# A macaron block in fp32: measures of later tiles, output-weight sums, token sums, one closing step and the last tile are each put elsewhere

## The chip, the cores and the metric

The kernel runs on one core of a Trainium2 chip. The metric is the device time of one execution in microseconds (us). Before the change three runs took 773.85, 774.33 and 774.45 us, median 774.33. The profile is one further execution of the same kernel.

Engines are named as in the profile: PE is the matrix engine TensorE (PEld its weight loads), DVE is VectorE, ACT is ScalarE, POOL is GpSimd, SP issues the DMAs. Each works through its own queue in order; they wait for one another through semaphores.

## The reference

`x` is 4 sequences of 256 tokens with 512 features, 1024 tokens in all. The block adds half a feed-forward, attention, and half a feed-forward again, each behind its own layer norm; both feed-forwards have the same weights.

```python
def _L0_attn_ref(x, wq, wk, wv, wo):       # 32 query heads, 8 key/value heads of 128
    q = (x @ wq).reshape(B, S, N_Q_HEADS, HEAD_DIM)
    k = (x @ wk).reshape(B, S, N_KV_HEADS, HEAD_DIM)
    v = (x @ wv).reshape(B, S, N_KV_HEADS, HEAD_DIM)
    q = _rope(q, pos); k = _rope(k, pos)
    scores = jnp.einsum('bqhgd,bshd->bhgqs', qg, k) * sm_scale
    allowed = (j <= i) & (j > i - SLIDING_WINDOW)          # window of 128
    attn = jax.nn.softmax(jnp.where(allowed, scores, neg), axis=-1)
    out = jnp.einsum('bhgqs,bshd->bqhgd', attn, v)
    return out.reshape(B, S, -1) @ wo

def _L0_ffn_ref(x, W_base, b_base, W_router, lora_A, lora_B):   # 8 experts of rank 16, top 2
    probs = softmax(xf @ W_router.T)
    w = one_hot(top 2) * (their probs, normed to a sum of 1)
    lora_out = jnp.einsum('ter,eor,te->to', h, lora_B, w) * SCALING   # h = xf by lora_A
    return x @ W_base.T + b_base + lora_out

x = x + 0.5 * ffn(layernorm(x))
x = x + attn(layernorm(x))
x = x + 0.5 * ffn(layernorm(x))
```

## The kernel before, in words

The 1024 tokens are 8 tiles of 128 rows. Tiles 0 to 3 (two sequences) are half 0 and tiles 4 to 7 half 1. All arithmetic is fp32. The rows `xt[t]` stay in SBUF from the first load to the last store.

*The first feed-forward* (`ffn`, called for both halves as `halves[0]` and `halves[1]`) is written as steps named by a letter and a tile of the half: M measures the mean and variance of a tile (`measure`: a statistics and an aggregate operation on DVE, a square root on ACT), X scales the rows with them (`scale`: on ACT in this feed-forward, on DVE in the others), T transposes them (`norm`: four transposes on PE, one copy on ACT), N does X and T, A multiplies by the adapters and the router, R computes the experts' shares, B is the base matmul of a tile into a PSUM bank (`base`, four matmuls of 512 columns), G gates the adapters, L leaves: the last matmul, by the adapters' second half, and an update of the tile on DVE (`leave`, L355 and L356). H and K are B's first and second two matmuls. A leave calls `then(t)`: in the first feed-forward `norm_later`, which measures the tile anew for the attention's norm and notes half 1's tiles in `behind`; in the second feed-forward `store`, which sends the tile out by a DMA on SP (L751).

*The projections* for q, k, v and the output use a scheme of seven products in place of eight (Strassen's, in Winograd's form). Each operand is cut in four quarters, sums of the quarters are made ahead, and products go into shared PSUM banks with additions on DVE between them. Sums of weights are made on POOL, four operations for each weight: `sum_weights` for q, k and v (L121) and `sum_o_weights` for the output (L126). Sums of tokens, `sum_tokens`, are four operations (L400), for half 0 on DVE and for half 1 by POOL and DVE in turn. Weight tiles and their sums (`wq`, `wqs`, `wos` and so on) have one buffer each, or two for `wo`, so new sums overwrite old ones.

`queries` gives the seven products of q as steps "1" to "7". A finished quarter goes through `rope`: one operation on DVE with the cosine (L380, tile `ra`), two with the sine (L382, tile `rb`), and a closing addition on POOL (L388). `ra` and `rb` have two buffers. With a list as `later`, the closing addition isn't issued but put on that list. Product 3's is always put on the list `ends` and issued by the caller later; product 5's was issued at once. `keys` and `project_values` do the same for k and v, in four parts called first, both, second and others.

*The attention* runs over 16 groups (half, key/value head), each with two units (one for each sequence of the half), 32 units in all. A unit u transposes its probabilities (L640), computes the scores of the unit after it (`scores`, L587 and L601), multiplies by v (`values`, L662), and starts the exponentials of the unit after (`exponentials`, L616 to L623). The four output products of a unit (`outputs`, L688, added on DVE at L698 and L705) are put on the queue `late` and worked off within the next unit. `normalize` (a reciprocal at L629 on DVE, two multiplications at L632 on POOL) closes a softmax. In units with b = 0 a string gives the order in which the seven products of the next group's q ("1" to "7") alternate with other steps ("n" normalize, "y" one of `late`, "t" transposes, "w" the output-weight sums, "v" and "k" early work of the first unit). Units with b = 1 do the k or v products for a following group, and the left-over work of half 1's norm: in every second such unit `scale` and `norm_attn` for the next two tiles of `behind`. Value units, those whose b = 1 part finishes v, are the ones with even n (n is the group's index plus 1).

*The second feed-forward* of half 0 runs in pieces inside the last units of half 1 (`fill`, `loose`); that of tiles 4 to 7 ends the program. The last line of orders reads:

```python
        (1, "N1 A0 A1 R"), (0, "G L0 L1"), (1, "B0 G H1 L0 K1 L1"),
```

Here number 1 is the pair of tiles 6 and 7, so the last tile's base matmul is cut in two, tile 6's leave stands between, and tile 7's leave, its update and its DMA are the program's end.

*What sets the order.* ACT and POOL run in the order in which the code is written, all through. So do PE and DVE until three units are left; the rest of theirs is ordered by a scheduler. So moving a call moves its instructions in the queue of every engine that it uses, and a wait of the first in a queue holds the rest. PSUM has four banks for matmuls (`mm_bank`) and four for scores and transposes (`score_bank`). Ahead of the first tile PE runs idle transposes of an identity (L166) until there is work.

The lines around the first feed-forward's end, which the change reorders:

```python
    tokens = sum_tokens(0, *(nc.vector,) * 4)
    for step in (1, 2, 3, 4):
        tokens[step]()
    sum_weights("k", *groups[0])
    sum_weights("q", *groups[0])
    for step in "L0 L1 B3".split():
        halves[1](step)
    first, both, second, others = keys(*groups[0])
```

Of the kernel before, what the change touches and what calls it, by code (L numbers as in the profile page):

```python
# [13 lines left out]
AF = mybir.ActivationFunctionType  # L14
ALU = mybir.AluOpType
# [23 lines left out]
def macaron_kernel(  # L39
# [122 lines left out]
    make_identity(nc, ident)  # L162

    idle = ps.tile([P, KC, P], F32, tag="s", bufs=4, name="idle")
    for n in range(21):
        nc.tensor.transpose(idle[:, n % KC, :], ident, ident)  # L166


# [68 lines left out]
    def scale(t, tag):  # L237
        if (tag, t) not in moments:
            measure(t, tag)
        mv, std = moments[tag, t]  # L240
        rstd = sb.tile([P, 1], F32, tag="rstd", bufs=4, name=f"rs_{tag}_{t}")
        nc.vector.reciprocal(rstd, std)
        xc = sb.tile([P, D], F32, tag="xc", bufs=3, name=f"xc_{tag}_{t}")
        if tag == "f1":
            shift = sb.tile([P, 1], F32, tag="shift", bufs=4, name=f"sh_{tag}_{t}")
            nc.vector.scalar_tensor_tensor(shift, mv[:, 0:1], -1.0, rstd, ALU.mult, ALU.mult)
            nc.scalar.activation(xc, xt[t], AF.Identity, bias=shift, scale=rstd)
        else:
            nc.vector.tensor_scalar(xc, xt[t], mv[:, 0:1], rstd, ALU.subtract, ALU.mult)
        moments[tag, t] = xc  # L250
# [49 lines left out]
    def ffn(tiles, tag, then):  # L300
        n, t0 = len(tiles), tiles[0]
        xf, po, state = {}, {}, {}

        def x_of(i, c):
            return xf[i // 2][:, c, ts(i % 2, P)]

        def enter(i, scaled=False):
            if i % 2 == 0:
                xf[i // 2] = sb.tile(
                    [P, KC, 2 * P], F32, tag="oT", bufs=4, name=f"xn_{tag}_{tiles[i]}"  # L310
                )
            norm(tiles[i], xf[i // 2], i % 2, tag, scaled)

        def look(i):
            measure(tiles[i], tag)

        def shape(i):
            scale(tiles[i], tag)

        def turn(i):  # L320
            enter(i, scaled=True)

        def narrow(i):
            t = tiles[i]
            if i == 0:
                state["hl"] = sb.tile([P, TPH, E * R + E], F32, tag="hl", name=f"hl_{tag}_{t0}")[:, :n, :]
            pa = score_bank(f"pa_{tag}_{t}")
            for c in range(KC):
                nc.tensor.matmul(  # L329
                    pa[:, : E * R + E], x_of(i, c), ar_sb[:, c, :],  # L330
                    start=(c == 0), stop=(c == KC - 1),
                )
            nc.scalar.copy(state["hl"][:, i, :], pa[:, : E * R + E])
            nc.gpsimd.tensor_tensor(xt[t], xt[t], half_bias, ALU.add)

        def shares():
            route(t0, n, state["hl"], tag)

        def base(i, chunks=range(KC)):
            if chunks[0] == 0:  # L340
                po[i] = mm_bank(f"po_{tag}_{tiles[i]}")
            for c in chunks:
                nc.tensor.matmul(po[i], x_of(i, c), wb_sb[:, c, :], start=(c == 0), stop=False)  # L343

        def gated():
            hl = state["hl"]
            pt = ps.tile([P, n, P], F32, tag="s", bufs=4, name=f"ph_{tag}_{t0}")
            for i in range(n):
                nc.tensor.transpose(pt[:, i, :], hl[:, i, : E * R], ident)
            state["ht"] = sb.tile([P, TPH, P], F32, tag="ht", bufs=1, name=f"ht_{tag}_{t0}")  # L350
            nc.scalar.copy(state["ht"][:, :n, :], pt)

        def leave(i):
            out, t = po.pop(i), tiles[i]
            nc.tensor.matmul(out, state["ht"][:, i, :], lb_sb, start=False, stop=True)  # L355
            nc.vector.scalar_tensor_tensor(xt[t], out, 0.5, xt[t], ALU.mult, ALU.add)  # L356
            then(t)

        steps = {
            "M": look, "X": shape, "T": turn, "N": enter, "A": narrow, "R": shares, "G": gated,  # L360
            "B": base, "H": lambda i: base(i, range(KC // 2)), "K": lambda i: base(i, range(KC // 2, KC)),
            "L": leave,
        }
        return lambda s: steps[s[0]](*(int(i) for i in s[1:]))

# [44 lines left out]
    def temp(name, at):  # L410
        return sb.tile([HD, TH], F32, tag=name, bufs=1, name=f"{name}_{at}")

    def queries(h, g, copy, later=None):

        state = {}

        qT[h, g] = sb.tile([HD, BPH, S // BLK, G, BLK], F32, tag="qT", name=f"qT_{h}_{g}")  # L420

        def product(n, bank=None):
            w, x = weights["qs", h, g][n - 1], xs[h][n - 1]
            new = bank is None
            if new:
                bank = mm_bank(f"q{n}_{h}_{g}")
            for j in range(2):
                for c in range(2):
                    nc.tensor.matmul(  # L429
                        bank[:, ts(j, S)], w[:, c, ts(j, HD)], x[:, c, :],  # L430
                        start=(new and j == 0 and c == 0), stop=(c == 1), skip_group_check=True,
                    )
            return bank

        def turn(b, j, src, later=None):
            rope(
                qT[h, g][:, b, :, j : j + 2, :], src, f"q_{h}_{g}_{b}_{j}",
                lambda t: t.rearrange("p (j e q) -> p e j q", j=2, q=BLK), later,
            )

        def first():
            state["p1"] = product(1)
            state["p1c"] = temp("p1c", f"q_{h}_{g}")
            copy(state["p1c"], state["p1"])

        def sixth():
            state["p6"], state["u2"] = product(6), temp("u2", f"q_{h}_{g}")
            add(state["u2"], state["p6"], state["p1c"])

        def seventh():  # L450
            state["p7"], state["v1"] = product(7), temp("v1", f"q_{h}_{g}")
            add(state["v1"], state["p7"], state["u2"])

        def fifth():
            state["p5"] = product(5)
            add(state["p6"], state["p5"], state["v1"])
            turn(1, 2, state["p6"])

        def second():
            turn(0, 0, product(2, state["p1"]))

        def fourth():
            bank = product(4, state["p7"])
            add(bank, bank, state["u2"])
            turn(0, 2, bank)

        def third():
            product(3, state["p5"])  # L470
            add(state["p5"], state["p5"], state["u2"])
            turn(1, 0, state["p5"], later)

        return {"1": first, "2": second, "3": third, "4": fourth, "5": fifth, "6": sixth, "7": seventh}
# [284 lines left out]
    def norm_later(t):  # L759
        if t >= TPH:  # L760
            behind.append(t)
        measure(t, "a")

# [16 lines left out]
    for h, order in (  # L782
        (0, "M0 M1 X0 X1 T0 T1 M2 A0 X2 M3 A1 T2 X3 B0 T3 A2 A3"), (1, "M0 M1 X0 X1"), (0, "B1"),
        (1, "T0 T1 M2 M3 X2"), (0, "R B2"), (1, "X3 T2"), (0, "B3"), (1, "T3"), (0, "G"),
        (1, "A0 A1 A2 A3"), (0, "L0 L1"), (1, "R"), (0, "L2 L3"), (None, "X0 X1 X2"), (1, "B0 B1 B2"),
        (None, "T0 T1 X3"), (1, "G"), (None, "T2 T3"),
    ):
        for step in order.split():
            (attn if h is None else halves[h])(step)
    tokens = sum_tokens(0, *(nc.vector,) * 4)  # L790
    for step in (1, 2, 3, 4):
        tokens[step]()
    sum_weights("k", *groups[0])
    sum_weights("q", *groups[0])
    for step in "L0 L1 B3".split():
        halves[1](step)
    first, both, second, others = keys(*groups[0])
    ends = []
    steps = queries(*groups[0], nc.scalar.copy, ends)
    first()  # L800
    both()
    for step in "L2 L3".split():
# [7 lines left out]
        if step == "4":  # L810
            load_q(*groups[1])
    sum_weights("q", *groups[1])
    ends.pop()()
    load_o(*groups[1])


# [24 lines left out]
    for u, (h, g, b) in enumerate(units):  # L841
# [12 lines left out]
        if b == 0 and n < len(groups):  # L854

            order = {0: "1n6kv2754t3w", 4: "1yn6a27cy5d4yte3yw"}[len(late)]
            steps = queries(*groups[n], nc.vector.tensor_copy, ends)
            steps |= {  # L860
                "y": lambda: run(late, 1), "n": lambda: normalize(ahead[0], ahead[2]),
# [12 lines left out]
        elif b == 1 and n + 1 < len(groups):  # L874
# [4 lines left out]
                more_tokens[4]()  # L879
            second()  # L880
            normalize(ahead[0], ahead[2])
            if n % 2 == 1 and (h, g) != groups[NKV]:
                sum_weights("v", *groups[n + 1])
            others()
            fill(left, 4)
            turned = [behind.popleft() for _ in range(2 if behind and n % 2 == 0 else 0)]
            for t in turned:
                scale(t, "a")
            if n % 2 == 0 and n + 2 < len(groups):
# [58 lines left out]
    f2 = [ffn(tiles(last[0], b, 1), "f2", store) for b in range(BPH)]  # L948
    for n, order in (
        (0, "N0 N1"), (None, 0), (None, 1), (0, "A0 A1 R B0"), (1, "N0"), (0, "B1"),  # L950
        (1, "N1 A0 A1 R"), (0, "G L0 L1"), (1, "B0 G H1 L0 K1 L1"),
    ):
        if n is None:
            out_project(*last, order, oT)
# [49 lines left out]
```

## Time and profile before

| | |
|---|---|
| median of three runs | 774.33 us |
| profiled execution | 773.88 us |
| its span, first to last instruction | 772.2 us |
| granted TensorE clock | 1.00 all through |
| idle transposes of PE at the start | to about 6.3 us |
| first base matmul (L343) | 10.89 us |
| first product of q (L429) | 58.56 us |
| first output product (L688) | 105.27 us |
| end of the last update on DVE | 769.18 us |
| last DMA: issue, first packet, landing | 769.21, 770.03, 771.21 us |

Times are read from the start of the span. An engine's row in the timeline gives the start, the duration, the engine and the line of the code, the operation with its tiles (out<-in), and in brackets how long the engine had been idle and what released it. A count behind an x means that so many instructions are drawn together. Part 6 of the page gives, for the DMAs, the time from issue to landing: 7.6 us for the base weights of 1024 KB, 5.5 for each q weight of 1024 KB, 2.0 for each output tile of 256 KB.

### The profile page before, as it was taken

Reading aid. Unit: us, or ns where it says so; the run is one execution under the profiler, and the core shown is the slowest. Engines: PE = TensorE matmul, PEld = TensorE weight load, DVE = VectorE, ACT = ScalarE, POOL = GpSimd, SP = SyncE. Lnnn points to the kernel's source line nnn. Section 1 sums busy time; section 2 is a strip of 40 time slices with the busy share of each in tenths; the row PEclk is TensorE's granted clock in tenths of the full one; section 3 lists DMA queues with packets and bytes.
Section 4 is the critical chain, followed back from the end, with each engine's and each line's share of the span. In section 5 each row is a group of like instructions: output and inputs, shape, how many; then the busy total and the mean of one; then the engine's idle time right before and its main releaser. Section 6 shows DMA issues by size and latency. Waiting matters only on the chain.

```text
span 772.2 us, 10908 instructions
## 1 busy us (share of the span) xinstructions
PE 764.5 (99%) x3809; PEld 617.4 (80%) x3809; DVE 538.7 (70%) x1307; ACT 213.9 (28%) x746; POOL 502.6 (65%) x540
## 2 busy tenths in 40 slices
PE   8999999999999999999999999999999999999998
PEld 6658888888888888888888888888888888877654
DVE  4487785857785877668677858586867768485673
ACT  5530232322223031322222232222141212223442
POOL 5452786866867595859585789669575957475411
PEclk9999999999999999999999999999999999999999
DMA  9301130303030302212030403030302011010001
GB/s 303 134 1 54 36 102 1 136 2 109 28 110 28 107 30 63 75 55 82 20 118 1 135 2 110 28 110 28 110 28 85 25 56 55 1 55 28 1 28 54
DMA packets 29335, 48.95 MB, mean 63 GB/s; under 512 B 1120, under 2 KB 10080, under 8 KB 29280
## 3 DMA queue, kind: packets, MB, share of 16 engines
q1 hardware_dynamic: 29280, 48.26, 18.5%
q8 instruction: 30, 0.49, 0.3%
q14 instruction: 25, 0.20, 0.1%
HBM read 46.15 MB, written 2.10 MB: 62 GB/s over the span
## 4 chain that ended last, share of the span: by engine, by line
PE 92%; DVE 4%; POOL 1%; issue 1%; ACT 0%; DMA 0%; DVEq 0%; POOLq 0%
PE y L688 24%; PE q L429 24%; PE ob L662 7%; PE k L486 6%; PE v L536 6%; PE po_f L343 5%; PE sb L601 4%; PE t L640 4%; PE sa L587 3%; PE oa L662 3%; PE pa_f L329 2%; PE po_f L355 1%; PE pt_f L258 1%; PE y L730 1%; DVE x L356 1%
## 5 line engine op out<-in xcount | busy, mean ns | idle before, releaser
L388 POOL TENSOR_TENSOR qT<-ra_q,rb_q 128x512 f32<-128x512 f32 x64 | 81.3, 1271 | 117.2 <-DVE rb_q L382 117.2
L382 DVE TENSOR_TENSOR rb_q<-q,sin_sb 64x512 f32<-64x512 f32 x128 | 88.1, 688 | 1.7
L644 ACT COPY p<-t 128x512 f32<-128x512 f32 x32 | 18.8, 586 | 212.9 <-PE t L640 212.9
L632 POOL TENSOR_TENSOR probs<-probs,sm 128x512 f32<-128x512 f32 x64 | 65.2, 1039 | 11.2 <-DVE sm L629 10.6
L688 PE MATMUL y<-wos,oT 128*128 128x256 f32 x248 | 63.9, 380 | 0.3 <-POOL wos L126 0.3
L688 PE MATMUL y<-wo,oT 128*128 128x256 f32 x248 | 63.7, 379 | 0.0
L688 PE MATMUL y<-wo,oTs 128*128 128x256 f32 x244 | 62.6, 379 | 0.0
L429 PE MATMUL q<-xs,wqs 128*128 128x256 f32 x256 | 60.6, 379 | 0.4 <-POOL wqs L121 0.4
L429 PE MATMUL q<-xs,wq 128*128 128x256 f32 x256 | 60.6, 379 | 0.2 <-DVE rb_k L382 0.2
L429 PE MATMUL q<-xa,wq 128*128 128x256 f32 x256 | 60.6, 379 | 0.0
L662 PE MATMUL ob<-p,v 128*128 128x512 f32 x128 | 60.2, 592 | 0.0
L380 DVE TENSOR_TENSOR ra_q<-q,cos_sb 128x512 f32<-128x512 f32 x64 | 44.3, 692 | 21.7 <-PE q L429 15.7
L429 PEld LDWEIGHTS q<-xa,wq 128*128 128x128 f32 x256 | 48.4, 190 | 12.8 <-issue 6.2
L343 PE MATMUL po_f<-wb_sb,xn_f 128*128 128x512 f32 x128 | 57.5, 593 | 0.0
L665 ACT COPY oT<-oa 128x512 f32<-128x512 f32 x32 | 18.7, 585 | 135.5 <-PE oa L662 135.5
L429 PEld LDWEIGHTS q<-xs,wqs 128*128 128x128 f32 x256 | 48.6, 190 | 7.4 <-POOL wqs L121 0.8
L429 PEld LDWEIGHTS q<-xs,wq 128*128 128x128 f32 x256 | 48.6, 190 | 7.1 <-issue 0.5
L688 PEld LDWEIGHTS y<-wo,oT 128*128 128x128 f32 x248 | 46.6, 190 | 6.0
L688 PEld LDWEIGHTS y<-wo,oTs 128*128 128x128 f32 x244 | 46.4, 190 | 6.3
L688 PEld LDWEIGHTS y<-wos,oT 128*128 128x128 f32 x248 | 45.6, 190 | 6.9 <-issue 1.0
L121 POOL TENSOR_TENSOR oTs<-oT 128x256 f32<-128x256 f32 x31 | 22.6, 731 | 40.6 <-ACT oT L665 40.5
L662 PEld LDWEIGHTS ob<-p,v 128*128 128x128 f32 x128 | 24.3, 190 | 30.6 <-issue 23.0
(182 smaller groups left out, 1711.5 us busy)
## 6 DMA issues: line engine op xcount, KB each, us to landing
wq<-in_wq_dram SPq DMA_DIRECT2D x16, 1024.0 KB, 5.5
wo<-in_wo_dram SPq DMA_DIRECT2D x16, 1024.0 KB, 5.0
wk<-in_wk_dram SPq DMA_DIRECT2D x8, 512.0 KB, 3.5
wv<-in_wv_dram SPq DMA_DIRECT2D x8, 512.0 KB, 3.5
x<-in_x_dram SPq DMA_DIRECT2D x8, 256.0 KB, 6.9
out_dram<-x SPq DMA_DIRECT2D x8, 256.0 KB, 2.0
wb_sb<-in_w_base_dram SPq DMA_DIRECT2D x1, 1024.0 KB, 7.6
ar_sb<-in_w_ar_dram SPq DMA_DIRECT2D x1, 272.0 KB, 5.0
```

The source lines that it names most:

```text
L343: nc.tensor.matmul(po[i], x_of(i, c), wb_sb[:, c, :], start=(c == 0), stop=False)
L380: nc.vector.tensor_tensor(twice(a), twice(src), angle(cos_sb), ALU.mult)
L382: nc.vector.tensor_tensor(twice(b[o : o + half, :]), twice(src[i : i + half, :]), angle(sin_sb[o : o + half, :]), ALU.mult,)
L388: nc.gpsimd.tensor_tensor(dst, view(a), view(b), ALU.add)
L429: nc.tensor.matmul(bank[:, ts(j, S)], w[:, c, ts(j, HD)], x[:, c, :], start=(new and j == 0 and c == 0), stop=(c == 1), skip_group_check=True,
L486: nc.tensor.matmul(dst, w[n - 1][:, c, :], x[n - 1][:, c, :], start=(start and c == 0), stop=(c == 1), skip_group_check=True,)
L536: nc.tensor.matmul(bank[:, i, :], x[n - 1][:, c, ts(i, P)], w[n - 1][:, c, :], start=(start and i == 0 and c == 0), stop=(c == 1), skip_gr ...
L601: nc.tensor.matmul(pb[:, at : at + P + BLK], q[:, NB + m], k[:, o + m * BLK : o + m * BLK + P + BLK], start=True, stop=True,)
L632: nc.gpsimd.tensor_tensor(w, w, sm[:, n : n + NB].unsqueeze(2).to_broadcast([P, NB, P]), ALU.mult)
L640: nc.tensor.transpose(pt[:, e, :, :], pr[:, n0 + e, :], ident)
L662: nc.tensor.matmul(po, v[:, 2 * b + n, cols], part, start=(n == 0), stop=(n == len(parts) - 1))
L688: nc.tensor.matmul(py[:, ts(i, D // 2)], lhs[n - 1][:, c, :], weights["os", h, g][n - 1][:, c, :], start=(i == 0 and c == 0), stop=(c == 1 ...
```

## The change

1. The start: 20 idle transposes in place of 21, and tile 0's scaling on ACT in two operations of 256 columns in place of one of 512.
2. Around the end of the first feed-forward: the weight sums for k and q come first in the code (POOL ran them in that order anyway), behind them now the output-weight sums of group 0, which were the last step ("w") of unit 0; then the leaves L0 and L1 of half 1, and only behind them the four token sums on DVE, which stood ahead.
3. `fifth` of the first group puts its closing addition on the list `ends` too. Both closings are now issued behind the q-weight sums of group 1; of the two only product 3's was so before.
4. Half 1's tiles are no longer measured in their leaves, but all four in unit 3 (n = 2, b = 1), behind `normalize`. Their scaling and transposes move from the units with n = 2 and 4 to those with n = 4 and 6.
5. The last tile is computed by column parts. H1 does columns 0 to 255 whole (four base matmuls, the adapters' matmul, update, DMA) in a bank of its own; K1 does the same for columns 256 to 511. L1 at the end falls away. `base` no longer takes parts.

```diff
-    for n in range(21):
+    for n in range(20):
         nc.tensor.transpose(idle[:, n % KC, :], ident, ident)
...
-            nc.scalar.activation(xc, xt[t], AF.Identity, bias=shift, scale=rstd)
+            for cols in (slice(0, D // 2), slice(D // 2, D)) if t == 0 else (slice(0, D),):
+                nc.scalar.activation(xc[:, cols], xt[t][:, cols], AF.Identity, bias=shift, scale=rstd)
...
+        def columns(i, cols):
+
+            bank, t = mm_bank(f"po_{tag}_{tiles[i]}_{cols.start}"), tiles[i]
+            part, xs = bank[:, : D // 2], xt[t][:, cols]
+            for c in range(KC):
+                nc.tensor.matmul(part, x_of(i, c), wb_sb[:, c, cols], start=(c == 0), stop=False)
+            nc.tensor.matmul(part, state["ht"][:, i, :], lb_sb[:, cols], start=False, stop=True)
+            nc.vector.scalar_tensor_tensor(xs, part, 0.5, xs, ALU.mult, ALU.add)
+            nc.sync.dma_start(out=out[ts(t, P), cols], in_=xs)
...
-            "B": base, "H": lambda i: base(i, range(KC // 2)), "K": lambda i: base(i, range(KC // 2, KC)),
-            "L": leave,
+            "B": base, "L": leave, "H": lambda i: columns(i, slice(0, D // 2)),
+            "K": lambda i: columns(i, slice(D // 2, D)),
...
         def fifth():
             state["p5"] = product(5)
             add(state["p6"], state["p5"], state["v1"])
-            turn(1, 2, state["p6"])
+            turn(1, 2, state["p6"], both_later)
...
     def norm_later(t):
         if t >= TPH:
             behind.append(t)
-        measure(t, "a")
+        else:
+            measure(t, "a")
...
+    sum_weights("k", *groups[0])
+    sum_weights("q", *groups[0])
+    sum_o_weights(*groups[0])
+    for step in "L0 L1".split():
+        halves[1](step)
     tokens = sum_tokens(0, *(nc.vector,) * 4)
     for step in (1, 2, 3, 4):
         tokens[step]()
-    sum_weights("k", *groups[0])
-    sum_weights("q", *groups[0])
-    for step in "L0 L1 B3".split():
-        halves[1](step)
+    halves[1]("B3")
     first, both, second, others = keys(*groups[0])
     ends = []
-    steps = queries(*groups[0], nc.scalar.copy, ends)
+    steps = queries(*groups[0], nc.scalar.copy, ends, ends)
...
     sum_weights("q", *groups[1])
-    ends.pop()()
+    for end in ends:
+        end()
+    ends.clear()
     load_o(*groups[1])
...
-            order = {0: "1n6kv2754t3w", 4: "1yn6a27cy5d4yte3yw"}[len(late)]
+            order = {0: "1n6kv2754t3", 4: "1yn6a27cy5d4yte3yw"}[len(late)]
...
             normalize(ahead[0], ahead[2])
+            if n == 2:
+                for t in behind:
+                    measure(t, "a")
...
-            turned = [behind.popleft() for _ in range(2 if behind and n % 2 == 0 else 0)]
+            turned = [behind.popleft() for _ in range(2 if behind and n in (4, 6) else 0)]
...
-        (1, "N1 A0 A1 R"), (0, "G L0 L1"), (1, "B0 G H1 L0 K1 L1"),
+        (1, "N1 A0 A1 R"), (0, "G L0 L1"), (1, "B0 G H1 L0 K1"),
```

## The prediction

> **What bounds the kernel now.** I read the page's busy times and chain first:
>
> ```profile
> PE 764.5 (99%) x3809; PEld 617.4 (80%) x3809; DVE 538.7 (70%) x1307; ACT 213.9 (28%) x746; POOL 502.6 (65%) x540
> PE 92%; DVE 4%; POOL 1%; issue 1%; ACT 0%; DMA 0%; DVEq 0%; POOLq 0%
> ```
>
> TensorE (PE) is busy 764.5 of 772.2 us, and the edits leave its work as it is. So time can come from only two places: moments in which PE stands still, and what lies before its first and after its last matmul. The waits of PE name the first:
>
> ```profile
> PE q L429 <- POOL wqs L121: 0.4, 1, 0.4
> PE k L486 <- DVE x L356: 0.3, 1, 0.3
> PE y L688 <- POOL wos L126: 0.3, 1, 0.3
> ```
>
> Each is one occurrence. The column gives idle time between modelled ends, which is too little. I measured start to start: in unbroken runs matmuls of 512, 256 and 128 columns follow each other every 0.429, 0.216 and 0.111 us; what exceeds that is lost. By this measure the rows below lose 0.49 at 55.74, 0.16 at 58.56, 0.59 at 83.75 and 0.44 at 105.27, and after each such start the second matmul comes 0.07 to 0.10 late too. All losses together, the start's included, are 8.4 us. Here are these stretches on PE, then POOL, then VectorE (DVE):
>
> ```profile
> 55.74 1.10 PE L486 MATMUL k<-xs,wks 128*128 128x256 f32 x4 [0.33 <-DVE x L356]
> 58.56 0.70 PE L429 MATMUL q<-xa,wq 128*128 128x256 f32 x2
> 83.75 1.13 PE L429 MATMUL q<-xs,wqs 128*128 128x256 f32 x4 [0.42 <-POOL wqs L121]
> 105.27 0.92 PE L688 MATMUL y<-wos,oT 128*128 128x256 f32 x3 [0.28 <-POOL wos L126]
> ```
>
> ```profile
> 49.72 1.26 POOL L121 TENSOR_TENSOR wq<-wq 128x512 f32<-128x512 f32 x1
> 66.69 1.27 POOL L388 TENSOR_TENSOR kT<-ra_k,rb_k 128x512 f32<-128x512 f32 x1 [15.71 <-DVE rb_k L382]
> 79.85 1.27 POOL L388 TENSOR_TENSOR qT<-ra_q,rb_q 128x512 f32<-128x512 f32 x1 [1.66 <-DVE rb_q L382]
> 82.42 1.27 POOL L121 TENSOR_TENSOR wqs<-wqs,wq 128x512 f32<-128x512 f32 x1
> 103.92 1.29 POOL L126 TENSOR_TENSOR wos<-wo,wos 128x512 f32<-128x512 f32 x1
> ```
>
> ```profile
> 50.05 1.48 DVE L400 TENSOR_TENSOR xs<-xa 128x512 f32<-128x512 f32 x1 [1.43 <-ACT xa L259]
> 51.57 0.69 DVE L400 TENSOR_TENSOR xs<-xa,xs 128x512 f32<-128x512 f32 x1
> 53.38 0.68 DVE L356 SCALAR_TENSOR_TENSOR x<-po_f,x 128x512 f32<-128x512 f32 x1
> 105.27 1.20 DVE L617 TENSOR_SCALAR nm<-mx 128x4 f32<-128x4 f32 x1
> 347.95 1.32 DVE L400 TENSOR_TENSOR xs<-xa,xs 128x512 f32<-128x512 f32 x1
> ```
>
> Three things are to be seen. The matmul at 83.75 starts as the second of four weight sums ends (82.42 + 1.27), the one at 105.27 as the last output-weight sum does. POOL idles 15.7 us before 66.69. And a DVE operation on two SBUF tiles costs 0.69 alone (51.57), but 1.48 (50.05) or 1.32 (347.95) when a POOL operation is running: at 50.05 POOL's 49.72 ends at 50.98, and DVE ends 0.55 later. The tail:
>
> ```profile
> 767.36 1.02 PE L355 MATMUL po_f<-lb_sb,ht_f 128*128 128x512 f32 x2
> 768.49 0.69 DVE L356 SCALAR_TENSOR_TENSOR x<-po_f,x 128x512 f32<-128x512 f32 x1 [1.88 <-PE po_f L355]
> 769.21 0.33 SPq L751 DMA_DIRECT2D out_dram<-x  x1
> ```
>
> **The change part by part** (minus is a gain).
>
> *Start, 20 idle transposes and a split activation:* the first base matmul starts at 10.89, when its 1 MB of weights land (10.84; 7.6 us from the issue at 3.20, page part 6), so what ends earlier before it only waits longer. One transpose fewer is 0.2 us at the 0.213 cadence there, the activation's first half some 0.35 earlier; -0.05, bounds -0.25 (weights would land earlier) to +0.1.
>
> *Token sums behind leaves L0 and L1, output-weight sums moved ahead.* Gain: k's product 6 waits at 55.74 for a bank freed by L1's leave, which stands behind four token sums. In the new order the leaves' updates run from 50.36 and end at 51.91, so that wait (0.49+0.07) goes. Token sums then run from 51.93. Four output-weight sums of 1.27 to 1.30, POOL's cadence 1.35, now run 51.0 to 56.4 in POOL's idle, beside the token sums. Cost between two ends. If DVE is never held, four steps of 0.61 end at 54.4. If it waits out one or two POOL operations, they end at 55.7 to 56.9. If the engines alternate one for one (1.3 for POOL, 0.3 more for DVE, as in 347.95 to 349.27 with POOL's next then stretched to 1.60), they end at 58.4. Behind them come k's u2 (0.42) and L2's update (0.69), whose bank q's product 1 needs; PE itself is ready at 57.83. Start of q then 57.98 (-0.58 against 58.56), or 59.5 (+0.94). Rows for both behaviours exist: of the pairs of small operations at L616/L617 the second met another POOL operation in 8 of 17. I take the middle, 57.05 for the last sum, start 58.16: **-0.40**.
>
> The row comes first here: 1.48 against 0.69. The Trainium skill, page "SBUF — State Buffer", section "SBUF: two separate sides", says the same and speaks against this edit: DVE and GpSimd share one port pair as an exclusive lock held for a whole instruction, and a DVE operation with two SBUF inputs stands still while GpSimd holds it. By that rule taken strictly, each side in turn, the sum would be the alternating rival's below.
>
> *Fifth's close behind the next query sums:* POOL's 1.27 at 79.85 no longer stands ahead of the four wqs sums. Their weights were issued at 73.97 and landed by 78.9; product 3, last reader of the old sums, is through at about 79.4. Two sums end at about 82.1, PE wants them at 83.16. So 0.59+0.10 go: **-0.69**, bounds -0.69 and -0.3: DVE's v (91.43, needed by product 4 at 92.48 on PE) has only 0.1 to spare and may take some back. The postponed close waits until 86; its buffers are wanted again at 89.3.
>
> *Output-weight sums out of unit 0:* 0.44+0.10 at 105.27 go, if nothing is late next. Next is product 7 of k, which needs u2, and this stands on DVE behind L617 (1.20 at 105.27, held by POOL). u2 now ends at 106.8; without the hold (0.16 instead of 1.20) and 1.0 us earlier by the gains above it ends at 104.75, held by one of POOL's oTs sums (0.73, rows at 146.32 and after) at up to 105.95, and PE, by then earlier too, wants it at 105.3. **-0.35**, bounds -0.55 and +0.1.
>
> *Measures of tiles 4 to 7 into unit 3:* four times 0.69+0.18 on DVE at a cadence of 0.83 = 3.3 us at about 149.9, where two idle spells of 1.25 and 0.87 and the two scalings moved out of this unit (152.78 to 154.65) give back 4.0. On ACT four square roots of 0.29 and two table loads of 1.28 (rows at the start) fall into 3.52 idle before 155.93 and, for the load back to exponentials, ahead of 164.00. The reciprocal at 166.90 then comes 1.3 late and with it u_q (167.84) by 0.6, ahead of 0.73 and 1.03 of DVE idle; the probabilities, ready at 170.5 instead of 169.3, are read by PE at 178.0. Cost **0**. If that cover is gone it is the whole addition on ACT, 4 x 0.29 + 2 x 1.28 = 3.7. In the leaves the measures removed free DVE time that bounds nothing but is in the times above. Eight transposes per pair of tiles (0.87 us) move from units 3 and 7 of the first half to 7 and 11: the same PE work, **0**; DVE's two scalings there take 0.76 to 0.81 each beside POOL, as before.
>
> *Last tile by columns:* the last update has 256 columns, 0.42 (such rows at L705) instead of 0.69: -0.27. Its DMA moves half: the packets of the last transfer ran 770.03 to 770.87, nine per queue at 85 ns; 1 KB packets in this trace took 46 ns, so 8 x 39 ns = -0.31. The rest stays: 0.82 from issue to first packet, 0.34 to landing, 0.97 to the end. Matmuls of 256 instead of 512 columns cost PE +0.03. The first half's transfer is issued more than 1 us earlier and is over. **-0.55**, bounds -0.70 and -0.25.
>
> Sum: -0.05-0.40-0.69-0.35+0-0.55 = -2.04. The profiled execution took 773.88 (span 772.2, 1.7 around it), which becomes 771.8; the runs' median, 774.33, lies 0.45 above that execution, so I predict **772.3**. All good ends together give -2.77 (771.6), all bad ones about +0.6 (774.9).
>
> **The rivals.**
>
> *Alternating:* token and weight sums take turns one for one, q starts at 59.5. Sum -2.04+0.40+0.94 = -0.70, 773.6. For it: 347.95 and its stretched POOL neighbour. Against: 51.57 follows 51.53 on DVE without a break, and half the L617 cases pass.
>
> *The waits are passed on:* product 7's u2 takes over the 105.27 wait (+0.1 instead of -0.35) and v at 91.43 keeps half of the 83.75 gain (-0.3). Sum -1.2, 773.1. For it: the 1.20 at 105.27; against: POOL has less to do there afterwards.
>
> *Starved, the slower side:* POOL's four sums stand back to back and DVE gets in only after the last, at 56.4. It decides from the point where DVE's request doesn't come between two POOL operations. Product 6 needs the second token sum (57.7, PE ready at 55.25), and q starts at about 60.4, +1.84. Sum -2.04+0.40+1.84 = +0.2, 774.5. Against: 347.95 got in after one.
>
> *Measures exposed, slower too:* the tables' changes in units 3 and 4 reach PE once the slack of 7.5 us before 178.0 or the copies of the old tiles' operands fail. Price 3.7: +1.7, 776.0. For it: ACT's copies at 152.04 and 155.93 feed PE's banks; against: that slack.
>
> **How the numbers follow.** Forecast 0.50, alternating 0.20, passed on 0.12, starved 0.08, measures exposed 0.10. The range 771.3 to 774.8 holds nearly all of the first three and half of the starved case. A measurement of this kernel can tell about 0.2% (1.55 us) from no change: under 772.78 is faster, over 775.88 slower. Faster: nine tenths of the forecast, two fifths of passed on, a fifth of alternating, 0.54. Slower: the exposed case and a little of the starved, 0.13. Same: the rest, 0.33.
>
> **What would show it.** Right: no wait of PE at the key products or at wqs and wos in unit 0; q's first product at 58.0 to 58.3; the last update 0.42 and the last transfer under 1.75 from issue to landing. Wrong: token sums of 1.3 and more in a row with q past 59; a PE wait for u_k near 105; a PE wait for v, xa or probs between 150 and 180; a first base matmul later than 10.9.

## The result, and the profile after

The changed kernel takes 772.34 us (median of 12 runs, 772.10 to 772.62). The kernel before, run beside it 12 times, takes 773.93. The ratio is 0.998, with a 95% interval of 0.9973 to 0.9988: 1.6 us faster, clear of the spread but just at the 0.2% that the prediction counted as a difference. The profiled execution took 772.62 (span 770.9) and was the slowest of the twelve; before it was 773.88 (span 772.2). Times of the experiments below are given as the difference to the kernel before, which ran beside each group of them.

The page's busy times and engines of the chain, after:

```profile
PE 764.1 (99%) x3818; PEld 619.1 (80%) x3818; DVE 536.4 (70%) x1308; ACT 217.3 (28%) x749; POOL 503.1 (65%) x540
PE 95%; DVE 3%; DMA 1%; issue 0%; SPq 0%; DVEq 0%
```

PE's work is all but as it was (764.1 us in place of 764.5), and POOL's and DVE's hardly differ. So the gain can only lie in PE's waits and in what stands before its first and behind its last matmul. The two largest waits of PE behind the idle transposes, after (engine, line, what it waited for: total, times, longest):

```profile
PE q L439 <- DVE x L356: 0.8, 1, 0.8
PE po_f L343 <- DMA wb_sb<-in_w_base_dram: 0.4, 1, 0.4
```

The waits for `wqs`, for `wos` and at k's product are gone. In their place stands one for the update of a leave, ahead of q's first product, and one for the base weights at the start; what else is left, of 0.3 and less each, stood before too. This is the stretch of the first on PE, DVE and POOL, after:

```profile
55.49 1.03 PE L496 MATMUL k<-xs,wks 128*128 128x256 f32 x4
59.01 1.99 PE L439 MATMUL q<-xa,wq 128*128 128x256 f32 x8 [0.78 <-DVE x L356]
```

```profile
52.07 0.93 DVE L410 TENSOR_TENSOR xs<-xa 128x512 f32<-128x512 f32 x1
53.03 1.64 DVE L410 TENSOR_TENSOR xs<-xa,xs 128x512 f32<-128x512 f32 x1
54.60 1.75 DVE L410 TENSOR_TENSOR xs<-xa 128x512 f32<-128x512 f32 x1
56.28 1.75 DVE L410 TENSOR_TENSOR xs<-xa,xs 128x512 f32<-128x512 f32 x1
58.28 1.27 DVE L356 SCALAR_TENSOR_TENSOR x<-po_f,x 128x512 f32<-128x512 f32 x2
```

```profile
51.18 1.27 POOL L126 TENSOR_TENSOR wos<-wo 128x512 f32<-128x512 f32 x1
52.53 1.60 POOL L126 TENSOR_TENSOR wo<-wo 128x512 f32<-128x512 f32 x1
54.20 1.60 POOL L126 TENSOR_TENSOR wos<-wo 128x512 f32<-128x512 f32 x1
55.88 1.59 POOL L126 TENSOR_TENSOR wos<-wo,wos 128x512 f32<-128x512 f32 x1
```

k's product at 55.49 no longer waits. But the four token sums, 0.69 each when alone, take turns with POOL's four sums: each ends about 0.55 after POOL's operation, POOL's next is stretched from 1.27 to 1.60, and the pair repeats every 1.67 us. The last token sum ends at 58.03, and u_k and L2's update, which frees q's bank, queue behind it. The tail, after:

```profile
767.23 0.59 PE L365 MATMUL po_f<-lb_sb,ht_f 128*128 128x256 f32 x2
767.86 0.42 DVE L366 SCALAR_TENSOR_TENSOR x<-po_f,x 128x256 f32<-128x256 f32 x1 [1.47 <-PE po_f L365]
```

From the last update's start to the end of the span it is 3.04 us (770.9 - 767.86); before it was 3.69 (772.18 - 768.49). The last transfer, 128 KB in place of 256, takes 1.7 from issue to landing in place of 2.0. The two products that had waited for weight sums, after, with the POOL row of the two closings that stand behind the sums now:

```profile
83.61 1.89 PE L439 MATMUL q<-xs,wqs 128*128 128x256 f32 x8
104.87 1.03 PE L698 MATMUL y<-wos,oT 128*128 128x256 f32 x4
85.30 2.51 POOL L398 TENSOR_TENSOR qT<-ra_q,rb_q 128x512 f32<-128x512 f32 x2
```

As the start varies with the landing of a DMA (below), stretches are best counted from the first base matmul, 10.89 before and 11.12 after. To q's first product: 47.67 before, 47.89 after, a loss of 0.22. From there to the first output product: 46.71 before (105.27 - 58.56), 45.86 after (104.87 - 59.01), a gain of 0.85. From there to the last update: 663.22 before, 662.99 after, -0.23, and the tail -0.65. With +0.23 at the start that is the 1.3 by which the spans differ.

### The profile page after: what moved, and what is told of

Its sections match the earlier page's. It is cut to its first block, busy times and chain, and to the rows that moved or that the text cites. A ratio compares the mean times of both kernels' runs of the same rounds, so it can differ in the third digit from the quotient of the medians.

```text
span 770.9 us, 10929 instructions
## 1 busy us (share of the span) xinstructions
PE 764.1 (99%) x3818; PEld 619.1 (80%) x3818; DVE 536.4 (70%) x1308; ACT 217.3 (28%) x749; POOL 503.1 (65%) x540
## 4 chain that ended last, share of the span: by engine, by line
PE 95%; DVE 3%; DMA 1%; issue 0%; SPq 0%; DVEq 0%
PE q L439 25%; PE y L698 24%; PE ob L672 7%; PE k L496 6%; PE v L546 6%; PE po_f L343 5%; PE sb L611 5%; PE sa L597 4%; PE t L650 4%; PE oa L672 4%; PE pa_f L330 2%; PE po_f L355 1%; DMA wb_sb<-in_w_base_dram 1%; PE y L740 1%; PE pt_f L259 1%; PE pv L581 1%
## 5 line engine op out<-in xcount | busy, mean ns | idle before, releaser
L343 PE MATMUL po_f<-wb_sb,xn_f 128*128 128x512 f32 x120 | 53.7, 593 | 0.4 <-DMA wb_sb<-in_w_base_dram 0.4
```

## The experiments

All are built from the changed kernel. The 95% intervals of the ratios reach 0.6 to 0.9 us to either side, so differences of 0.4 to 0.8 us between two of these kernels are not settled by the ratios alone. Where such a difference is read, it rests on the profile rows beside it as well.

**Output-weight sums behind the key closings.** Two theories on the 0.22 lost ahead of q: POOL's sums hold up the token sums, or the new order alone puts them in L2's way.

```diff
-    sum_o_weights(*groups[0])
     for step in "L0 L1".split():
...
     second()
     others()
+    sum_o_weights(*groups[0])
```

> The changed kernel with one move: group 0's four output-weight sums on POOL behind the two key closings (about 70.6) in place of behind the query sums (51.2). Theory (the token sums lose their time to POOL's sums beside them, 0.93 to 1.75 each in place of 0.69): the four token sums take 0.69 each and end at about 54.7, q's first product starts 47.1 us after the first base matmul (changed kernel 47.89, before 47.67) with no wait for an update at L356, and the time is 0.8 below the changed kernel: 771.5. Rival (the new order alone, tokens ahead of u_k and of L2's update, sets q's start): still 47.9, 772.3. Second rival (POOL then closes the queries late and the sums for group 1's queries with it): q early, but a wait for wqs near 83 of 0.5 and more: 772.0 to 772.5.

Measured: 771.32, 2.30 below the kernel before (ratio 0.9969, 0.9958 to 0.998), so 0.7 better than the change. DVE and POOL in this kernel:

```profile
51.46 0.68 DVE L410 TENSOR_TENSOR xs<-xa 128x512 f32<-128x512 f32 x1
52.18 0.69 DVE L410 TENSOR_TENSOR xs<-xa,xs 128x512 f32<-128x512 f32 x1
53.39 0.68 DVE L410 TENSOR_TENSOR xs<-xa,xs 128x512 f32<-128x512 f32 x1
```

```profile
69.56 1.27 POOL L126 TENSOR_TENSOR wos<-wo 128x512 f32<-128x512 f32 x1
73.61 1.27 POOL L126 TENSOR_TENSOR wos<-wo,wos 128x512 f32<-128x512 f32 x1
74.84 2.49 POOL L398 TENSOR_TENSOR qT<-ra_q,rb_q 128x512 f32<-128x512 f32 x2
78.75 1.27 POOL L121 TENSOR_TENSOR wqs<-wq 128x512 f32<-128x512 f32 x1 [1.42 <-PE q L439]
```

The same four token sums in the same order take 0.68 to 0.69, and q starts 47.07 after the first base matmul, in place of 47.89. POOL's sums fill the gap between the key and the query closings, and POOL still idles 1.42 before the wqs sums, so nothing is late behind them. The order alone is refuted as the cause; so is the second rival. This kernel is faster than the one before and the changed one.

**Output-weight sums back in unit 0.**

```diff
-    sum_o_weights(*groups[0])
...
-            order = {0: "1n6kv2754t3", 4: "1yn6a27cy5d4yte3yw"}[len(late)]
+            order = {0: "1n6kv2754t3w", 4: "1yn6a27cy5d4yte3yw"}[len(late)]
```

> The changed kernel with the output-weight sums put back as the last step of unit 0, all else as changed. Theory: lead-in as without POOL beside the tokens (q's first product at 47.1 after the first base matmul, -0.8), and the wait of the first output product for wos near 105 is back (+0.54): about 772.1. Rival (order alone): q still at 47.9, wait back: 772.9.

Measured: 772.01, 1.61 below the kernel before. q starts at 47.10, and the old wait is back on PE:

```profile
104.04 1.13 PE L698 MATMUL y<-wos,oT 128*128 128x256 f32 x4 [0.28 <-POOL wos L126]
```

Start to start it is 0.444 again and 0.10 behind it. So the early sums, as the change places them, gain 0.5 here and lose 0.7 to 0.8 in the lead-in: that edit as a whole is worth nothing or less, and its two halves are told apart.

**Product 5's closing at once again.**

```diff
-    steps = queries(*groups[0], nc.scalar.copy, ends, ends)
+    steps = queries(*groups[0], nc.scalar.copy, ends)
```

> The changed kernel with product 5's closing addition issued at once again, ahead of the sums for group 1's queries. Theory: the wait for wqs at the sixth product of group 1's q is back with 0.59 and 0.10, the 0.19 at its second product (behind the held L627) goes: +0.5, 772.85. Rival (the gain was passed on to later waits): within 0.2 of the changed kernel, 772.2 to 772.5.

Measured: 772.54, 1.08 below the kernel before, 0.5 worse than the change. The wait for wqs is back with 0.58, and the 0.19 that the changed kernel loses at product 2 of this q, start to start, is gone. That 0.19 is a wait for a copy on DVE: the copy ends at 87.20, 0.05 before the product starts. It stands behind an operation that takes 1.20 in place of 0.16 while POOL's two closings run from 85.30. The rows of the changed kernel:

```profile
85.40 1.20 DVE L627 TENSOR_SCALAR nm<-mx 128x4 f32<-128x4 f32 x1
86.52 0.68 DVE L454 COPY p1c_q<-q 128x512 f32<-128x512 f32 x1
87.25 1.99 PE L439 MATMUL q<-xa,wq 128*128 128x256 f32 x8
```

**The last tile in one piece again** (`base` in two parts, L1 at the end).

```diff
-        (1, "N1 A0 A1 R"), (0, "G L0 L1"), (1, "B0 G H1 L0 K1"),
+        (1, "N1 A0 A1 R"), (0, "G L0 L1"), (1, "B0 G H1 L0 K1 L1"),
```

> The changed kernel with the last tile in one piece again. Theory (the last update is 0.27 shorter, the last DMA's packets 0.31 and the last matmul of 256 columns ends 0.2 sooner): from the last update's start to the end of the span 3.69 again in place of 3.04, +0.78, 773.1. Rival (the DMA's time is fixed and only the update counts): +0.27 to 0.4, 772.65.

Measured: 772.90, 0.72 below the kernel before, 0.87 worse than the change. In its tail the update takes 0.69 again, and it starts 3.72 before the end of the span (771.0):

```profile
767.28 0.69 DVE L357 SCALAR_TENSOR_TENSOR x<-po_f,x 128x512 f32<-128x512 f32 x1 [1.88 <-PE po_f L356]
```

The rival of a DMA of fixed time is out: it allowed 0.27 to 0.4, and the last transfer takes 2.0 again in place of 1.7.

**The start as before.**

```diff
-    for n in range(20):
+    for n in range(21):
...
-            for cols in (slice(0, D // 2), slice(D // 2, D)) if t == 0 else (slice(0, D),):
-                nc.scalar.activation(xc[:, cols], xt[t][:, cols], AF.Identity, bias=shift, scale=rstd)
+            nc.scalar.activation(xc, xt[t], AF.Identity, bias=shift, scale=rstd)
```

> The changed kernel with the start as before: 21 idle transposes, tile 0 scaled in one operation of 512. Theory (the base weights' landing, 7.2 to 7.9 us after their issue in the runs so far, sets the first base matmul, the forecast's term of 0.05): first base matmul within 0.1 of the landing, and the time 1.5 to 1.6 below the kernel before, as the changed kernel's 1.6. Rival (in most executions the weights land by 10.5, and then PE's own way is what the split shortens): first base matmul at 10.85 to 10.9 with the weights long there, 1.25 to 1.35 below the kernel before.

Measured: 772.04, 1.63 below the kernel before, as the change (1.59). In its profiled execution the weights landed 7.2 us after their issue, and PE started on them at once:

```profile
10.43 1.98 PE L342 MATMUL po_f<-wb_sb,xn_f 128*128 128x512 f32 x4
```

Over the profiled executions of kernels with the new start the landing took 7.2 to 7.9 us and the first base matmul came between 10.52 and 11.15. So the edits at the start are worth nothing that these runs can tell, and the late 11.12 in the profile of the changed kernel is its DMA, not its code.

**Measures back in the leaves, with the change, and with the better place of the output-weight sums.** The measures were forecast to cost nothing in either place.

```diff
         if t >= TPH:
             behind.append(t)
-        else:
-            measure(t, "a")
+        measure(t, "a")
...
-            if n == 2:
-                for t in behind:
-                    measure(t, "a")
...
-            turned = [behind.popleft() for _ in range(2 if behind and n in (4, 6) else 0)]
+            turned = [behind.popleft() for _ in range(2 if behind and n % 2 == 0 else 0)]
```

> The changed kernel with half 1's measures back in the leaves and the scalings back in units with n = 2 and 4. Forecast's theory (the measures cost nothing in either place): 1.6 below the kernel before, as the changed kernel. Rival (in the new order two measures, 1.66 on DVE, stand ahead of the token sums, and these end about as much later, beside POOL's sums until 56 and free of them after): last token sum at about 58.6 to 59.3, q's first product 48.5 to 49.1 after the first base matmul in place of 47.9, 0.5 to 1.0 below the kernel before.

> The kernel with the output-weight sums behind the key closings (2.3 below the kernel before) with the measures back in the leaves. Theory (the measures matter only while POOL holds up the token sums; free, these end at 55.5 and q at 57.6 doesn't wait): q's first product at 47.1 after the first base matmul, 2.2 to 2.4 below the kernel before. Rival (the measures' place is worth time by itself): a wait for an update at L356 is back, 1.5 to 2.0 below.

Measured: with the change's other edits 772.47, 1.20 below the kernel before, 0.4 worse than the change; with the output-weight sums behind the key closings 771.29, 2.38 below, the same as without (2.30). In the first the measures push the token sums to 53.55, the second is held by POOL and k waits for it, 0.68 start to start:

```profile
52.73 0.69 DVE L230 BATCH_NORM_STATS2 st_a<-x 128x6 f32<-128x512 f32 x1
53.55 0.66 DVE L410 TENSOR_TENSOR xs<-xa 128x512 f32<-128x512 f32 x1
54.25 1.64 DVE L410 TENSOR_TENSOR xs<-xa,xs 128x512 f32<-128x512 f32 x1
```

The last token sum ends at 58.16, not 58.6 or later, because POOL is done by then; q starts at 48.17. So the measures' move has no worth of its own; it only takes the edge off the collision that the other edit makes. The later start of q, 48.17 against 47.89, accounts for 0.3 of the 0.4; this edit takes back the later scalings too, and the two weren't run apart.

**Token sums ahead of the leaves again, output-weight sums still early.**

```diff
-    for step in "L0 L1".split():
-        halves[1](step)
     tokens = sum_tokens(0, *(nc.vector,) * 4)
     for step in (1, 2, 3, 4):
         tokens[step]()
-    halves[1]("B3")
+    for step in "L0 L1 B3".split():
+        halves[1](step)
```

> The changed kernel with the token sums ahead of the leaves L0 and L1 again, the output-weight sums still early. Theory (the engines take turns): token sums of 1.2 to 1.75 each from 50 to about 56.5, the updates of L0 and L1 behind them, a wait of PE for the update at the key products from about 55.5 to 58, q's first product 49.3 to 50.5 after the first base matmul: 0.2 below to 1.0 above the kernel before. Rival (PE has cover enough, the position against the leaves doesn't matter): 47.7 to 48.0, 1.6 below.

> The kernel with the token sums ahead of the leaves once more, one look. Its eleven times lay at 774.4 to 774.6 (four) and at 775.4 to 776.6 (seven), and its profiled execution was of the upper group. Theory (the upper group is the executions in which PE's matmuls run at half rate for some 3.5 us behind its 2.65 us of idleness): if this execution is of the lower group, the matmuls from 58 to 62 follow each other every 0.216 and 0.429 and q's first product starts about 50 after the first base matmul; if of the upper group, it shows the half rate again. Rival (the spread has another cause): the half rate in a lower one, or none in an upper one.

Measured: 775.89 (774.37 to 776.55), 2.2 above the kernel before (1.0024, 1.0015 to 1.0033), more than either theory had; only the lower group of its times, 0.7 to 1.0 above, lies where the theory of turns put it. A further execution took 774.11. The token sums, beside POOL's, take 1.47 to 1.75, and PE stands still for 2.65 us, then goes on. The first profiled execution (span 774.7), then the second (772.4):

```profile
57.47 1.13 PE L496 MATMUL k<-xa,wk 128*128 128x256 f32 x4 [2.65 <-DVE x L356]
58.43 1.84 PE L496 MATMUL k<-xs,wks 128*128 128x256 f32 x4
60.07 2.80 PE L355 MATMUL po_f<-lb_sb,ht_f 128*128 128x512 f32 x4
62.84 1.99 PE L439 MATMUL q<-xa,wq 128*128 128x256 f32 x8
```

```profile
56.81 1.13 PE L496 MATMUL k<-xa,wk 128*128 128x256 f32 x4 [2.65 <-DVE x L356]
57.78 1.03 PE L496 MATMUL k<-xs,wks 128*128 128x256 f32 x4
58.64 1.88 PE L355 MATMUL po_f<-lb_sb,ht_f 128*128 128x512 f32 x4
60.52 1.99 PE L439 MATMUL q<-xa,wq 128*128 128x256 f32 x8
```

The second shows what the order costs: q 49.91 after the first base matmul, as the theory of turns said (49.3 to 50.5), so with the output-weight sums early the place behind the leaves is worth 2.0. In the first, matmuls behind the same wait run at half rate for 3.4 us, from about 58.6 to 62.0, and q starts at 51.69, 1.8 later still. The granted clock between 58.60 and 62.00 is 0.51 there, and 1.00 in the second. The two executions lie on the two sides of the gap between the groups; that all the others divide in this way is likely but not shown.

**One more wait taken away.** On the faster kernel, the one with the output-weight sums behind the key closings, product 5 of the first group's q and its addition were issued ahead of the sine operations of product 4's rope, since product 3 waits 0.43 for that addition.

```diff
         nc.vector.tensor_tensor(twice(a), twice(src), angle(cos_sb), ALU.mult)
+        if between:
+            between()
...
-        def fifth():
+        def fifth_sum():
             state["p5"] = product(5)
             add(state["p6"], state["p5"], state["v1"])
+
+        def fifth():
+            if both_later is None:
+                fifth_sum()
             turn(1, 2, state["p6"], both_later)
...
-            turn(0, 2, bank)
+            turn(0, 2, bank, None, None if both_later is None else fifth_sum)
```

> The kernel with the output-weight sums behind the key closings (2.3 below the kernel before), and in the first group's q product 5 and its addition issued between the cosine and the sine operations of product 4's rope. Theory (the wait of 0.43 and 0.10 of product 3 is for an addition that stands on DVE behind product 4's rope of 2.1; ahead of its sine part it is 0.6 to 1.4 sooner): the wait at about 76.7 is 0 to 0.1, 2.7 to 2.85 below the kernel before. Rival (the sine part, 0.7 later, closes product 4 later on POOL and holds up the first scores): a new wait of 0.2 to 0.7 at the scores (L597), 2.1 to 2.5 below.

Measured: 771.92, 1.66 below the kernel before, 0.64 worse than without the edit and less than either expectation had. The wait of 0.43 is gone, but the scores start 0.27 late, and two waits further on are new or longer:

```profile
78.59 1.16 PE L603 MATMUL sa<-kT,qT 128*128 128x32 f32 x8
86.30 1.99 PE L441 MATMUL q<-xa,wq 128*128 128x256 f32 x8 [0.29 <-DVE p1c_q L456]
92.08 1.99 PE L441 MATMUL q<-xs,wq 128*128 128x256 f32 x8 [0.33 <-DVE v_q L420]
```

Start to start the two are 0.45 (0.19 without the edit) and 0.49 (none). DVE works without a break from 75.8 to 86.2 there; the wait of 0.43 had been the place where PE let it catch up.

## Why the prediction was right, and where its steps were not

The time came out (772.3 forecast, 772.34 measured), and so did the direction, but that they lie so close is luck. The forecast took 2.04 off 774.33, the median of three runs; twelve runs of that kernel beside the changed one have a median of 773.93, and the measured gain is 1.59. The starting point was 0.40 too high and the gain 0.45 too large. Within the sum, the lead-in, the wait for wqs and the start came out 0.86 worse than forecast, the wait for wos and the last tile 0.51 better. The measured gain lies between the forecast's 2.04 and the 1.2 of the waits passed on. Of the signs of being wrong that were named, two appeared: token sums of 1.3 and more in a row with q past 59 (59.01), and a first base matmul later than 10.9 (11.12, for its DMA).

*Lead-in, forecast -0.40, measured +0.22.* This step failed. It took the middle between one POOL operation waited out (last token sum at 55.7) and strict alternation (58.4), and called alternation a rival with 0.20. In the profile the engines alternate, in each of the four pairs. The rows held against alternation didn't bear on it: at 51.57 POOL had no further operation until 66.69, and the small operations that passed at L617 take 0.16 alone, the token sums 0.69. The rival's own size was too high (q 48.61 after the first base matmul, measured 47.89), since the first token sum met only the end of a POOL operation and took 0.93 where the rival had 1.6; the other three ended 1.67 apart. The wait for L1's update went as forecast. That the collision with POOL and not the order costs it is shown by moving POOL's sums alone: 0.7 to 0.8. What the text took from "SBUF — State Buffer", section "SBUF: two separate sides", of the Trainium skill, that the one engine stands still while the other holds the shared ports for a whole instruction, agrees with these rows in the mechanism and the sign: each DVE sum ends only after the POOL operation beside it. Taken strictly it would not have given the better size: its +0.94 is 0.72 off the measured +0.22, the forecast 0.62. A pair takes 1.67 here, less than the 1.96 that 0.69 and 1.27 make one after the other.

*The wait for wqs, forecast -0.69 with -0.3 as the bad end, measured -0.5.* The wait went whole. 0.19 of it came back, not at product 4 by way of v_q, which the forecast watched, but three products earlier, at product 2, behind the L627 row that POOL's closings now hold.

*The wait for wos, forecast -0.35, measured -0.54.* The value was too cautious; the good end, -0.55, came true. The hold on DVE fell on L626 (the L616 of the kernel before) with 0.73 in place of the 1.20 at L617, u_k ended at 105.96, and k's product ran at 106.60 without a wait.

*Measures, forecast 0.* Right for units 3 and 4: PE shows no wait there, and the table loads of 1.28 appear as forecast. But the statement that the freed DVE time bounds nothing was wrong in the order that the change makes: it is worth up to 0.4 there and nothing once POOL's sums are elsewhere.

*Start, forecast -0.05, measured 0* within what the runs can tell (1.63 against 1.59 below the kernel before).

*Last tile, forecast -0.55, measured -0.87.* The mechanism was right and the size too small, outside its bounds of -0.70 and -0.25. Update and packets were counted; what was left out is that the last matmul also has half the columns, so that the update starts 0.41 after that matmul's start in place of 0.70.

The measured terms, +0.22 - 0.5 - 0.54 + 0 + 0 - 0.87, give -1.7, against -1.59 of the medians.

## What to carry to other kernels

Idle time of POOL is not free ground: ask what DVE does with two SBUF operands in the same stretch and place POOL's work beside DVE work that reads PSUM, as the sums behind the key closings do: beside them the query's additions and the rope on DVE took 0.68 to 0.70 each, as when alone. Where a term has two ends and a row for each, don't take the middle: look how many operations stand back to back on both sides. Here the two engines took turns wherever sums of 0.69 and of 1.27 were both waiting. And ask whether a row held against a rival meets the rival's condition. A wait of PE on a chain in which DVE never rests need not be time to be had; taking it away here moved it to three later places and cost 0.64.

## What the runs showed of the hardware that was not expected

A wait of PE of 2.65 us was followed in one execution, about 1 us after PE was back at work, by 3.4 us of matmuls at half rate (512 columns 0.85 apart in place of 0.43, granted clock 0.51 in place of 1.00), and in another execution of the same kernel, with the same wait, by none. The waits under 1 us in these profiles were not followed by it. What decides between the two executions is not shown. The Trainium skill, page "TensorE: Matmul & The Clock Gate", section "Part 1: The HAM clock gate (the "warmup" mystery)", tells of a gate that halves the clock after an idle window of about 3.4 us and opens again after a busy one, in windows that run freely. The 3.4 us at half rate, and that only one of two equal waits is hit, agree with this; that 2.65 us of idleness were enough doesn't, taken by the length it gives.
